# A two-layer graph network on one core: new costs, three dependences and a new order in the planner

## The chip, the core and the metric

The kernel runs on one core of a Trainium2 chip. Its engines work from queues of their own: PE (TensorE, matrix products), DVE (VectorE), ACT (ScalarE), POOL (GpSimd) and SP (SyncE, which here issues nearly all DMA transfers). [...] The metric is the device time of one execution in microseconds (us), as the median of several runs; lower is better. Everything is float32.

## The reference

The input x has 64 batches of 256 tokens with 512 features; adj is one 256 x 256 mask for all. Two layers follow each other, each with a residual and a layer norm:

```
q, k, v = x@Wq+bq, x@Wk+bk, x@Wv+bv                      (8 heads of 64)
attn    = softmax(q k^T / 8, masked with -1e9 where adj is 0)
x       = layernorm(x + (attn v) @ Wo + bo)
h       = x @ W
e       = leaky_relu(h a1 (by rows) + h a2 (by columns), 0.2) * adj
x       = layernorm(x + elu(softmax(e) h + beta h))
```

## The kernel before, in words

**Tiling and rounds.** Batches go in pairs m = 0 to 31; batch s = 0 or 1 is half of a pair. A pair shares x transposed (xT) and the products q, k and v; all else is done per batch. The pieces of work on PE have names: "x" (a gate, see below), "q", "k", "v", and per half "scores00" to "scores31" (head pair c of half s), "sums" (softmax denominators), "mix" (weights times v), "o" (the Wo product), "logits", "attention", "spread" (second-layer weights times x) and "u" (product with W). The table ROUND is the order of these pieces within a round; LATER says how many rounds after (or, negative, before) its own number a pair's piece is done, so that a round mixes pieces of three or four pairs. The last pair is done by the table FINISH, of (piece, how many pairs before the last). take_turn (L601) turns these tables into PE's order.

**Products.** project (L429) computes a matrix product in seven half-size products in place of eight, with sums and differences of quarters. It calls pe(1), pe(5), pe(2), pe(6), pe(3), pe(4), pe(7) in that order. Four PSUM accumulators serve them: chain, cross, second and fourth; for narrow products (o, u, spread) second and fourth are two halves of one tile, "both" (ps_pair in the profile). gather (L480) or onto (L934) move the quarters to SBUF: for q, k, v, spread and u a copy on ACT and an addition on DVE, for o two additions on DVE. token_sums (L408) makes the operand's sums on POOL (xS, oS, yS). PSUM has 8 slots (tag "ps"); x's sums have a single one ("xP").

**Attention.** scores (L758) uses 64-row tiles of PE (mode "rows" in the planner); for each head DVE adds the mask (L774), ACT exponentiates (L776), POOL adds two key halves (L779), and DVE transposes and reduces (L785, L786). denominators (L790) is one 32-column product, L794, then a reciprocal on DVE (L797) and two steps of DMA through DRAM, rows_all and inv_all (L801, L805). mixed (L734) uses 64-column tiles (mode "columns", L744); its result is scaled on DVE (L858). norm (L573) is two passes with row sums on ACT (L580), three small operations on POOL (L591 to L593) and a scaling pass on ACT (L597).

**The planner.** Nothing is emitted at once: plan.op (L90) records engine, an estimated duration, the emitting function, what is read and written, and which buffers are claimed. place (L121) then simulates the engines with these numbers and a fixed latency LAG per engine, and picks operations one by one, by possible start and by a due time that is counted back from PE's order. The order that comes out is emitted engine by engine; on the chip each engine runs its own list in order. Only the last OPEN = 70 products may be reordered on PE. An operation of PE with duration 0 emits nothing: it is a gate, at which buffers of that stage are claimed ("x", "logits", "attention"). A DVE operation with mode "two" isn't planned at the same time as one of POOL, since they share a port ("port" in place). Durations and latencies only shape the order: true waits come from the data.

Of the kernel before, what the change touches and what calls it, by code (L numbers as in the profile page):

```python
# [22 lines left out]
ROUND = ("mix1", "sums1", "scores30", "scores20", "scores00", "scores10", "logits0", "v", "spread1", "o1", "u1", "x",  # L23
         "mix0", "sums0", "scores31", "scores21", "scores01", "scores11", "attention0", "q", "attention1", "logits1",
         "k", "spread0", "o0", "u0")

LATER = {"sums1": 1, "mix1": 1, "scores00": 0, "scores10": 0, "scores20": 0, "scores30": 0, "spread1": 2, "v": 0,
         "u1": 2, "attention0": 1, "sums0": 0, "mix0": 0, "scores01": 0, "scores11": 0, "scores21": 0, "scores31": 0,
         "o1": 1, "x": -2, "logits1": 1, "q": -1, "spread0": 1, "o0": 0, "attention1": 1, "u0": 1, "k": -1, "logits0":
         1}  # L30

FINISH = (("logits0", 1), ("mix1", 1), ("sums1", 1), ("scores00", 0), ("scores30", 0), ("scores20", 0), ("v", 0),
          ("scores10", 0), ("spread1", 2), ("logits1", 1), ("o1", 1), ("scores31", 0), ("sums0", 0), ("u1", 2),
          ("attention0", 1), ("mix0", 0), ("scores01", 0), ("u0", 1), ("scores21", 0), ("attention0", 0),
          ("spread0", 1), ("u1", 1), ("o0", 0), ("spread1", 1), ("spread0", 0), ("logits1", 0), ("logits0", 0),
          ("sums1", 0), ("scores11", 0), ("attention1", 0), ("o1", 0), ("attention1", 1), ("mix1", 0), ("u0", 0),
          ("spread1", 0), ("u1", 0))
# [25 lines left out]
class Plan:  # L63
# [11 lines left out]
    SWITCH = 100.0  # L75
# [14 lines left out]
    def op(self, engine, ns, fn, reads=(), writes=(), mode=None, claims=(), first=False):  # L90
# [24 lines left out]
        self.ops.append((engine, ns, fn, deps, bufs, mode))  # L115
        if engine == "PE":
            self.turns.append((self.turn, n))
        if first:
            self.first = n

    def place(self):  # L121
# [10 lines left out]
        for n in reversed(turns):  # L132
            t += self.SWITCH if ops[n][5] != mode else 0.0
            mode = ops[n][5]
            due[n] = t
            t += ops[n][1]
        for n in reversed(range(len(ops))):
            e, ns = ops[n][:2]
            if e != "PE":
                late = [due[u] - ns - (self.LAG[e] if ops[u][0] != e or e == "SP" else 0.0)  # L140
                        for u in users[n] if due[u] is not None]
                due[n] = min(late, default=None)
# [5 lines left out]
        for n in reversed(range(len(ops))):  # L148
            e, ns = ops[n][:2]
            rest[n] = ns + max((rest[u] + (self.LAG[e] if ops[u][0] != e or e == "SP" else 0.0) for u in users[n]),  # L150
                               default=0.0)
# [17 lines left out]
        while len(order) < len(ops):  # L169
            best = None  # L170
            for e, cand in ready.items():
# [3 lines left out]
                for n in cand:  # L175
                    start = max(now[e], base[n])
                    _, ns, _, _, bufs, m = ops[n]
# [15 lines left out]
                    cost = self.SWITCH if e == "PE" and m != mode else 0.0  # L193
# [7 lines left out]
            _, ns, _, _, bufs, m = ops[n]  # L201
            if e == "PE" and m != mode:
                start += self.SWITCH
                mode = m
            if e == "PE":
                turns.remove(n)
            if e == "POOL" or m == "two":
                port = start + ns
# [5 lines left out]
            now[e] = start + ns  # L214
            end[n] = start + ns + self.LAG[e]
# [6 lines left out]
            for u in users[n]:  # L222
                need[u] -= 1
                lag = 0.0 if ops[u][0] == e and e != "SP" else self.LAG[e]
                base[u] = max(base[u], start + ns + lag)
                if not need[u]:
                    ready[ops[u][0]].append(u)
# [9 lines left out]
def gnn_two_layers(ctx: ExitStack, tc: tile.TileContext, x, adj, Wq, bq, Wk, bk, Wv, bv, Wo, bo, W, a, beta, out):  # L237
# [107 lines left out]
    def transposed_mask():  # L345
# [8 lines left out]
        plan.op("DVE", 690, lambda: nc.vector.tensor_scalar(  # L354
# [19 lines left out]
    def streamed(w, w_dram, name):  # L374
# [16 lines left out]
        def fetch(n):  # L391

            piece = sb("piece", [2, F], f"{name}_{n}")
            if n in raw:
                i, c = raw[n]
                plan.op("SP", 800, lambda: nc.sync.dma_start(
                    piece[A], w_dram[2 * c * P:2 * (c + 1) * P, half(i)].rearrange("(c p) f -> p c f", p=P)), [],
                    [piece])
            else:
                k = {5: 1, 6: 2, 7: 3, 3: 4}[n]  # L400
                plan.op("SP", 800, lambda: nc.sync.dma_start(piece[A].rearrange("p c f -> p (c f)"), kept[k - 1]),
                        [(kept, k)], [piece])
# [26 lines left out]
    def project(left, right, by_feature, claims, copy, add, inner=2, width=P, first=False):  # L429
# [21 lines left out]
        ns = 224 * inner * 2 if by_feature and width == P else 435 * inner * (width // P)  # L451
# [3 lines left out]
        def pe(n, to, start, after=()):  # L455
# [3 lines left out]
            plan.op("PE", ns, lambda: product(n, acc(), start), sides[n][1] + right[n - 1][1] + list(after), [to],  # L459
                    claims=claims)  # L460
# [19 lines left out]
    def gather(quarter, bias=None, wide=False):  # L480

        def copy(q, acc):
# [4 lines left out]
            for f in range(2):  # L487
                plan.op("ACT", 370, lambda f=f: nc.scalar.activation(  # L488
# [3 lines left out]
        def add(q, acc):  # L492
            (dst, key), (src, acc) = quarter(q), acc[::-1]
            plan.op("DVE", 690 if wide else 420, lambda: nc.vector.tensor_add(dst(), src(), dst()), [acc, key], [key])  # L494
# [33 lines left out]
    def residual_bias():  # L528
        bo_sb = for_now(bo, 0, "bo")
        acc, part = ps([D], "ps_b"), sb("half", [D], "bv_wo")  # L530
        for c in range(C):
            plan.op("DVE", 690, lambda c=c: nc.vector.scalar_tensor_tensor(
# [4 lines left out]
            acc[A], ones[:, 16:17].to_broadcast([P, P]), part[A], start=True, stop=True), [part], [acc], claims=[res_sb])  # L537
        plan.op("DVE", 690, lambda: nc.vector.tensor_add(res_sb[A], acc[A], bo_sb[A]), [acc, bo_sb], [res_sb])
# [6 lines left out]
    def second_layer_constants():  # L545
# [4 lines left out]
        for i in range(2):  # L550
            col, a_sb = st(C, "col"), for_now(a, i * D, "a")
            for c in range(C):
                junk = sb("half", [D], "junk")
                plan.op("DVE", 780, lambda c=c, junk=junk, col=col, a_sb=a_sb: nc.vector.scalar_tensor_tensor(  # L554
# [9 lines left out]
            plan.op("DVE", 690, lambda i=i, row=row: nc.vector.tensor_copy(wa_sb[:, i, :], row[A]), [row], [(wa_sb, i)])  # L564
# [8 lines left out]
    def norm(X, ts):  # L573
# [4 lines left out]
        def total(i, t, func, to, bias):  # L578
            junk = sb("half", [D], "junk")
            plan.op("ACT", 700, lambda: nc.scalar.activation(  # L580
# [5 lines left out]
        plan.op("DVE", 110, lambda: nc.vector.tensor_scalar(mean[A], sums[A], -1.0 / D, None, ALU.mult), [sums], [mean])  # L586
# [8 lines left out]
        plan.op("POOL", 1000, rsqrt, [sq, mean], [rs, nm])  # L595
# [12 lines left out]
    def pair(m, at, general=False):  # L608
# [28 lines left out]
        def blocks(s):  # L637
# [3 lines left out]
            for f in range(4):  # L641
                plan.op("SP", 700, lambda f=f: nc.sync.dma_start(
                    xb[f * 32:(f + 1) * 32].rearrange("p c (b i) -> p c b i", i=32), rows[f]), [], [(xb, f)])
# [47 lines left out]
    def batch(m, s, qT, kT, V, dram, general):  # L691
# [12 lines left out]
        def finish(ts, us, u, mode):  # L704

            for t in ts:
                m = sb("half", [D], "m")
                plan.op("ACT", 640, lambda t=t, m=m: nc.scalar.activation(m[A], u(t), AF.Exp), us(t), [m])
                plan.op("DVE", 700, lambda t=t: nc.vector.scalar_tensor_tensor(
                    X[:, t, :], u(t), 0.0, X[:, t, :], op0=ALU.max, op1=ALU.add), us(t), tokens(t), mode=mode)  # L710
                plan.op("DVE", 700, lambda t=t, m=m: nc.vector.scalar_tensor_tensor(  # L711
                    X[:, t, :], m[A], 1.0, X[:, t, :], op0=ALU.min, op1=ALU.add), [m], tokens(t), mode="two")
            norm(X, ts)
            for t in ts:
                plan.op("SP", 700, lambda t=t: nc.sync.dma_start(dram(out, s)[:, t, :], X[:, t, :]), tokens(t), [])
# [10 lines left out]
        plan.op("SP", 2800, lambda: nc.sync.dma_start(X[A], dram(x, s)), [], tokens(0) + tokens(1))  # L726
        for t in range(NT):
            plan.op("POOL", 1270, lambda t=t: nc.gpsimd.tensor_tensor(X[:, t, :], X[:, t, :], res_sb[A], ALU.add),  # L728
# [5 lines left out]
        def mixed(pT, g, onto):  # L734
# [12 lines left out]
            plan.op("PE", 1740, pe, [(V, (g, j)) for j in range(NT)] + pT[4 * g:4 * g + 4], [acc],  # L747
# [3 lines left out]
        def attention_by_keys():  # L751
# [6 lines left out]
            def scores(c):  # L758
# [11 lines left out]
                plan.op("PE", 870, pe, [(m, (c // 2, j)) for m in (qT, kT) for j in range(NT)], acc, mode="rows",  # L770
                        claims=pT[2 * c:2 * c + 2] + ([] if last else [both[c]]))
                for i in range(2):
                    h = 2 * c + i
                    plan.op("DVE", 690, lambda h=h, i=i: nc.vector.tensor_add(pT[h][A], acc[i][A], maskT_sb[A]),  # L774
# [402 lines left out]
```

## Time and profile before

| What | Value |
|---|---|
| median of 3 runs | 2688.45 us (2688.29 to 2689.46) |
| profiled execution, its own time | 2692.57 us |
| its span, first to last instruction | 2690.8 us |
| mean granted clock of PE | 0.997 |
| busy: PE, PE weight loads | 2662.2, 2252.2 us |
| busy: DVE, ACT, POOL | 2212.4, 1483.6, 1688.5 us |
| DMA | 301.21 MB, mean 112 GB/s |

The profile comes from one execution. A line of a timeline gives start, duration, engine, line of code, operation, what is written and read, and how many instructions of a kind follow each other. A matmul's duration includes its pipeline, so the next one starts before its end; what one costs is read from start to start. In the list of waits each line is: who waited, for whom, total us, how often, the longest. "PEld" is the loading of weights into PE. The engine named as the one that ended a wait is inferred.

### The profile page before, as it was taken

The page shows a single profiled execution, that of the slowest core. Times are in us where ns is not written, and L with a number is a line of the kernel's source. Part 1 is how long each engine was busy: PE and PEld are TensorE (multiplying, and loading weights), DVE is VectorE, ACT ScalarE, POOL GpSimd, SP SyncE. Part 2 cuts the span into 40 slices and gives each one's busy share as a digit, 9 for nine tenths or more (in the row PEclk, how much of TensorE's full clock was granted, in tenths as well). Part 3 has the DMA queues.
Part 4 walks back from the last instruction along what each step waited for, and adds up shares of the span by engine and source line. Part 5 has one row for each costly group of instructions (what it writes and reads, how often), then busy time and mean ns, then how long its engine had stood idle before and what let it go on. Part 6 is the DMA issues. An engine that isn't in the chain of part 4 may idle for free.

```text
span 2690.8 us, 45707 instructions
## 1 busy us (share of the span) xinstructions
PE 2662.2 (99%) x15037; PEld 2252.2 (84%) x15037; DVE 2212.4 (82%) x4188; ACT 1483.6 (55%) x3457; POOL 1688.5 (63%) x2254
## 2 busy tenths in 40 slices
PE   8999999999999999999999999999999999999997
PEld 7888888888888888888888888888888888888875
DVE  7878788888888888887878878888888788887886
ACT  3446556455565565564655655556546556455565
POOL 5765666665666655766556666566665666665654
PEclk9999999999999999999999999999999999999998
DMA  8435443454433545334544335443354543453321
GB/s 231 108 99 129 122 122 80 100 138 116 126 96 80 134 120 130 111 78 113 134 116 124 86 96 134 120 126 103 77 126 126 124 116 81 106 138 97 91 79 45
DMA packets 583227, 301.21 MB, mean 112 GB/s; under 512 B 409416, under 2 KB 513864, under 8 KB 582984
## 3 DMA queue, kind: packets, MB, share of 16 engines
q1 hardware_dynamic: 582856, 298.20, 43.1%
q8 instruction: 124, 2.03, 0.3%
q14 instruction: 119, 0.97, 0.1%
q0 software_dynamic: 128, 0.01, 0.0%
HBM read 245.63 MB, written 52.48 MB: 111 GB/s over the span
## 4 chain that ended last, share of the span: by engine, by line
PE 97%; DVE 1%; DMA 0%; issue 0%; ACT 0%; POOL 0%; SPq 0%; POOLq 0%; DVEq 0%
PE ps_chain L448 34%; PE ps_cross L448 22%; PE ps_pair L448 10%; PE ps_sc L767 9%; PE ps_pv L744 8%; PE ps_second L448 6%; PE ps_fourth L448 6%; PE ps_plain L513 0%; DMA xin<-in_x_dram 0%; DVE junk L959 0%; DMA row<-line 0%; PE ps_den L794 0%; DVE junk L554 0%; DVE x L711 0%; PE ps_plain L508 0%
## 5 line engine op out<-in xcount | busy, mean ns | idle before, releaser
L779 POOL TENSOR_TENSOR both<-pT 128x256 f32<-128x256 f32 x504 | 382.6, 786 | 76.8 <-ACT pT L776 74.6
L774 DVE TENSOR_TENSOR pT<-ps_sc,maskT_sb 128x512 f32<-128x512 f32 x512 | 318.3, 676 | 22.3 <-PE ps_sc L767 22.3
L776 ACT ACTIVATE pT<-pT 128x512 f32<-128x512 f32 x512 | 294.1, 624 | 30.9 <-DVE pT L774 30.8
L591 POOL TENSOR_SCALAR rs<-sq 128x2 f32<-128x2 f32 (+1 forms) x130 | 26.2, 202 | 404.8 <-ACT junk L580 402.2
L580 ACT ACTIVATE junk<-x 128x512 f32<-128x512 f32 x256 | 161.2, 630 | 190.4 <-DVE x L936 153.4
L959 DVE SCALAR_TENSOR_TENSOR junk<-x,wa_sb 128x512 f32<-128x512 f32 x256 | 213.8, 862 | 37.6 <-ACT x L597 36.6
L767 PE MATMUL ps_sc<-qT,kT 64*128 64x256 f32 x2048 | 239.6, 383 | 1.8 <-DVE kT L494 1.4
L597 ACT ACTIVATE x<-x,nmr,rs 128x512 f32<-128x512 f32 x256 | 202.6, 810 | 63.6 <-POOL nmr L593 63.6
L744 PE MATMUL ps_pv<-pT,v 128*64 128x256 f32 x2048 | 235.1, 382 | 0.0
L767 PEld LDWEIGHTS ps_sc<-qT,kT 64*128 64x128 f32 x2048 | 192.9, 187 | 25.9 <-DVE kT L494 1.8
L744 PEld LDWEIGHTS ps_pv<-pT,v 128*64 128x64 f32 x2048 | 141.4, 137 | 86.3 <-issue 20.9
L580 ACT ACTIVATE junk<-x,mean 128x512 f32<-128x512 f32 x256 | 183.8, 719 | 9.0 <-DVE mean L586 9.0
L419 POOL TENSOR_TENSOR oS<-oT 128x256 f32<-128x256 f32 x126 | 92.2, 732 | 138.1 <-DVE oT L858 133.2
L785 DVE STREAM_TRANSPOSE flip<-both 128x512 f32<-128x512 f32 x252 | 174.9, 694 | 4.4 <-DVE part L786 0.5
L786 DVE TENSOR_REDUCE part<-flip 128x16 f32<-128x512 f32 x252 | 172.1, 683 | 6.5
L728 POOL TENSOR_TENSOR x<-x,res_sb 128x512 f32<-128x512 f32 x128 | 177.3, 1406 | 0.0
L997 POOL TENSOR_TENSOR e<-e,adj_sb 128x512 f32<-128x512 f32 (+1 forms) x66 | 82.4, 1249 | 140.2 <-DVE e L994 140.2
L485 ACT COPY u<-ps_chain 128x256 f32<-128x256 f32 x126 | 45.0, 357 | 215.3 <-PE ps_chain L448 215.2
L488 ACT ACTIVATE kT<-ps_chain,bk_sb 128x256 f32<-128x256 f32 x128 | 53.8, 472 | 168.6 <-PE ps_chain L448 168.6
L1068 POOL TENSOR_TENSOR att_sums<-attT 128x128 f32<-128x128 f32 x126 | 70.7, 561 | 120.2 <-DVE attT L1032 114.4
L448 PE MATMUL ps_chain<-sw_sb,yS 128*128 128x256 f32 x504 | 132.4, 385 | 0.0
L936 DVE TENSOR_TENSOR x<-x,ps_chain 128x256 f32<-128x256 f32 x252 | 100.2, 417 | 38.0 <-PE ps_chain L448 32.2
(248 smaller groups left out, 7306.5 us busy)
## 6 DMA issues: line engine op xcount, KB each, us to landing
x<-in_x_dram SPq DMA_DIRECT2D x64, 512.0 KB, 3.7
out_dram<-x SPq DMA_DIRECT2D x128, 256.0 KB, 2.1
inv_all<-rows_all SPq DMA_DIRECT2D x126, 256.0 KB, 4.8
xin<-in_x_dram SPq DMA_DIRECT2D x248, 128.0 KB, 3.9
wq_sums<-wq_sums SPq DMA_DIRECT2D x124, 256.0 KB, 2.9
wk_sums<-wk_sums SPq DMA_DIRECT2D x124, 256.0 KB, 4.2
wq_sums<-in_L_gnn_Wq_dram SPq DMA_DIRECT2D x93, 256.0 KB, 4.1
wk_sums<-in_L_gnn_Wk_dram SPq DMA_DIRECT2D x93, 256.0 KB, 4.3
```

Source lines behind the costliest of these rows:

```text
L448: nc.tensor.matmul(dst[:, f, :], lhs, rhs, start=start and f == 0 and c == 0, stop=c == inner - 1, skip_group_check=True)
L580: plan.op("ACT", 700, lambda: nc.scalar.activation(junk[A], X[:, t, :], func, bias=mean[:, i:i + 1] if bias else 0.0, accum_out=to[:, i:i ...
L597: plan.op("ACT", 810, lambda i=i, t=t: nc.scalar.activation(X[:, t, :], X[:, t, :], AF.Identity, bias=nm[:, i:i + 1], scale=rs[:, i:i + 1] ...
L728: plan.op("POOL", 1270, lambda t=t: nc.gpsimd.tensor_tensor(X[:, t, :], X[:, t, :], res_sb[A], ALU.add), [res_sb], tokens(t))
L744: nc.tensor.matmul(acc[r * HD:(r + 1) * HD, i, :], V[:, 2 * k + s, h * HD:(h + 1) * HD], pT[h][:, k, :], start=k == 0, stop=k == NT - 1)
L767: nc.tensor.matmul(acc[j][:, k, :], kT[r:r + HD, c, key_blk(k)], own(qT, r, c), start=True, stop=True)
L774: plan.op("DVE", 690, lambda h=h, i=i: nc.vector.tensor_add(pT[h][A], acc[i][A], maskT_sb[A]), [acc[i], maskT_sb], [pT[h]])
L776: plan.op("ACT", 620, lambda h=h: nc.scalar.activation(pT[h][A], pT[h][A], AF.Exp, scale=1.0 / HD ** 0.5), [pT[h]], [pT[h]])
L779: plan.op("POOL", 725, lambda h=h, i=i: nc.gpsimd.tensor_tensor(both[c][:, i, :], pT[h][:, 0, :], pT[h][:, 1, :], ALU.add), [pT[h]], [(bot ...
L785: plan.op("DVE", 640, lambda: nc.vector.transpose(turned[A], both[c][A]), [both[c]], [turned])
L786: plan.op("DVE", 600, lambda: nc.vector.tensor_reduce(part[:, 2 * c:2 * c + 2, :], turned[A].rearrange("p i (q k) -> p i q k", k=32), AX.X ...
L959: plan.op("DVE", 780, lambda t=t, i=i, junk=junk: nc.vector.scalar_tensor_tensor(junk[A], X[:, t, :], 1.0, wa_sb[:, i, :], op0=ALU.mult, o ...
```

## The change

No arithmetic changes, and no operation or transfer is added or taken away. What changes is the planner and the order that it gives:

- ROUND, LATER and FINISH are new tables. In a round, q of the next pair stands between o1 and u1; the denominators stand ahead of the mix; attention0 and attention1 stand together among the scores of half 1; logits1 behind k; two scores of half 0 end a round and two begin the next. x is prepared one round later than before. The residual bias's product follows ROUND's "x" in round 0, so it moves to a place between two scores.
- An operation may have its own latency ("lag"): SP's transfers have a short occupation and a latency by kind. AFTER is a latency between dependent operations of one engine; KEPT is the end part of an operation in which its engine is already free.
- A change of PE's mode costs by the mode that is left (200 ns from "rows", else 100); gates no longer count as a change; a restart of PE after a wait costs AGAIN = 100. The denominators have a mode "one".
- Dependences: product 4 of project also counts as writing the other half of its PSUM tile, so that it waits in the plan for that half's reader; z (L988) counts as an operation that shares the port with POOL; operations of one engine that depend on each other keep AFTER between them.
- Some fifty durations are set anew.

```diff
-ROUND = ("mix1", "sums1", "scores30", "scores20", "scores00", "scores10", "logits0", "v", "spread1", "o1", "u1", "x",
-         "mix0", "sums0", "scores31", "scores21", "scores01", "scores11", "attention0", "q", "attention1", "logits1",
-         "k", "spread0", "o0", "u0")
+ROUND = ("scores20", "x", "scores10", "v", "logits0", "spread1", "o1", "q", "u1", "sums0", "mix0", "scores11",
+         "scores01", "attention0", "attention1", "scores31", "scores21", "k", "logits1", "spread0", "o0", "u0",
+         "sums1", "mix1", "scores00", "scores30")
...
-FINISH = (("logits0", 1), ("mix1", 1), ("sums1", 1), ("scores00", 0), ("scores30", 0), ("scores20", 0), ("v", 0),
...
+FINISH = (("logits0", 1), ("attention0", 1), ("scores20", 0), ("v", 0), ("spread1", 2), ("scores10", 0), ("o1", 1),
...
     LAG = {"PE": 260.0, "DVE": 70.0, "ACT": 70.0, "POOL": 90.0, "SP": 4200.0}
-    SWITCH = 100.0
+    KEPT = {"PE": 0.0, "DVE": 80.0, "ACT": 95.0, "POOL": 40.0, "SP": 0.0}
+    AFTER = {"PE": 0.0, "DVE": 30.0, "ACT": 30.0, "POOL": 80.0}
+    SWITCH = {None: 100.0, "rows": 200.0, "columns": 100.0, "sums": 100.0, "one": 100.0}
+    AGAIN = 100.0
...
+    def _lag(self, n, u):
+        e = self.ops[n][0]
+        return self.AFTER[e] if self.ops[u][0] == e and e != "SP" else self.ops[n][6]
...
-                    cost = self.SWITCH if e == "PE" and m != mode else 0.0
+                    cost = 0.0
+                    if e == "PE" and ns:
+                        cost = self.SWITCH[mode] if m != mode else self.AGAIN if start > now[e] else 0.0
...
-                port = start + ns
+                port = start + ns - self.KEPT[e]
...
-            now[e] = start + ns
-            end[n] = start + ns + self.LAG[e]
+            now[e] = start + ns - self.KEPT[e]
+            end[n] = start + ns + lag
...
-            plan.op("PE", ns, lambda: product(n, acc(), start), sides[n][1] + right[n - 1][1] + list(after), [to],
-                    claims=claims)
+            plan.op("PE", ns, lambda: product(n, acc(), start), sides[n][1] + right[n - 1][1] + list(after),
+                    [to] + list(after), claims=claims)
...
-                plan.op("ACT", 370, lambda f=f: nc.scalar.activation(
+                plan.op("ACT", 470, lambda f=f: nc.scalar.activation(
...
-        plan.op("POOL", 1000, rsqrt, [sq, mean], [rs, nm])
+        plan.op("POOL", 1250, rsqrt, [sq, mean], [rs, nm])
...
-                    stop=True), [part, fold_sb], [acc], mode="columns", claims=[inv])
+                    stop=True), [part, fold_sb], [acc], mode="one", claims=[inv])
...
-                    plan.op("SP", 1000, spread, [(rows_all, b)], [(everywhere, i)])
+                    plan.op("SP", 660, spread, [(rows_all, b)], [(everywhere, i)], lag=4700)
...
-            plan.op("DVE", 480, lambda t=t: nc.vector.tensor_scalar(
-                z[:, t, :], row[A], sv[:, t, 1:2], None, ALU.add), [row, (sv, (0, t))], [(z, t)])
+            plan.op("DVE", 430, lambda t=t: nc.vector.tensor_scalar(
+                z[:, t, :], row[A], sv[:, t, 1:2], None, ALU.add), [row, (sv, (0, t))], [(z, t)], mode="two")
```

## The prediction

> **What bounds the kernel now.** First the page: busy time per engine, then the chain that ended last.
>
> ```profile
> PE 2662.2 (99%) x15037; PEld 2252.2 (84%) x15037; DVE 2212.4 (82%) x4188; ACT 1483.6 (55%) x3457; POOL 1688.5 (63%) x2254
> PE 97%; DVE 1%; DMA 0%; issue 0%; ACT 0%; POOL 0%; SPq 0%; POOLq 0%; DVEq 0%
> ```
>
> TensorE (PE) sets the end, but "busy" hides small losses: ends of matmuls are modelled and overlap the next start. So I count from start to start. In the chain of waits the scores of batch 1 of two neighbouring rounds begin at
>
> ```profile
> 1906.47 3.65 PE ps_sc L767 x32
> ...
> 1989.10 3.65 PE ps_sc L767 x32
> ```
>
> so a round (one pair of batches) takes 82.63 us. Next the timeline of PE inside that round:
>
> ```profile
> 1926.26 1.03 PE L448 MATMUL ps_cross<-wo_sb,oT 128*128 128x256 f32 x4
> 1927.12 1.03 PE L448 MATMUL ps_pair<-wo_sb,oT 128*128 128x256 f32 x4
> ...
> 1928.85 1.03 PE L448 MATMUL ps_cross<-so_sb,oT 128*128 128x256 f32 x4
> 1929.95 1.10 PE L448 MATMUL ps_pair<-wo_sb,oS 128*128 128x256 f32 x4
> 1930.89 1.03 PE L448 MATMUL ps_chain<-so_sb,oS 128*128 128x256 f32 x4
> ...
> 1934.34 1.03 PE L448 MATMUL ps_chain<-sw_sb,yS 128*128 128x256 f32 x4
> 1935.35 1.13 PE L448 MATMUL ps_cross<-sw_sb,yT 128*128 128x256 f32 x4
> 1936.31 1.03 PE L448 MATMUL ps_pair<-w_sb,yS 128*128 128x256 f32 x4
> 1937.34 1.13 PE L448 MATMUL ps_chain<-sw_sb,yS 128*128 128x256 f32 x4
> 1938.40 3.67 PE L744 MATMUL ps_pv<-pT,v 128*64 128x256 f32 x32
> 1941.90 0.25 PE L794 MATMUL ps_den<-fold_sb,part 128*64 128x32 f32 x2
> 1942.08 3.72 PE L767 MATMUL ps_sc<-qT,kT 64*128 64x256 f32 x32
> 1945.74 1.99 PE L448 MATMUL ps_chain<-xT,wq_sums 128*128 128x256 f32 x8
> ```
>
> An undisturbed product of four matmuls steps by 0.864 (1926.26 to 1927.12). Here two products of o1 take 1.10 + 0.94, so 0.31 too long. Four of u1 take 1.01 + 0.96 + 1.03 + 1.06 = 4.06, which is 0.60 over 3.46; 0.09 of it is a change of tile shape (below), 0.51 is stall. Together 0.82 us a round. Starts in other rounds show the same in o1/u1, first at 194 us, and none in o0/u0. The list of waits agrees in count; the engines behind it come from the DVE and ACT timelines:
>
> ```profile
> PEld ps_pair L448 <- POOL yS L419: 12.5, 28, 0.4
> PEld ps_chain L448 <- ACT u L485: 11.5, 29, 0.4
> 1929.39 0.41 DVE L936 TENSOR_TENSOR x<-x,ps_pair 128x256 f32<-128x256 f32 x1
> 1934.31 0.63 ACT L580 ACTIVATE junk<-x 128x512 f32<-128x512 f32 x1 [1.12 <-DVE x L936]
> 1934.94 0.35 ACT L485 COPY u<-ps_cross 128x256 f32<-128x256 f32 x1
> ```
>
> The o1 wait is put down to POOL, but POOL's yS ended at 1929.54 and the next weight load began at 1929.92, just after DVE's read of the first half of ps_pair ended at 1929.80: product 4 writes the other half of that PSUM tile. The planner knew no such dependence. The u1 wait is ACT: the norm of o1 stood ahead of the copies of u1 and was itself waiting for DVE.
>
> **What the Trainium skill says.** "TensorE: Matmul & The Clock Gate", Architectural detail: ACT and DVE are strict FIFOs; the trace agrees, ACT sat 1.12 us idle with a ready copy behind L580. "TensorEngine Tiling (Array Packing)", Key Properties: changing the tiling mode drains TensorE; the trace agrees, 0.09 to 0.20 us a change. "GPSIMD Engine Reference", Specifications: SBUF interfaces are shared with VectorE operations in two-port mode; L988 (z), which the old plan thought free of this, runs 336 to 1432 ns.
>
> **The change, part by part.**
>
> *Cost of a change of mode.* From starts at 1240.76 to 1250.88: into the mix 0.95 - 0.86 = 0.09, its first pair 3.51 - 3.46 = 0.05, the denominators 0.18 - 0.05 (two 32-column matmuls) = 0.13, scores 3.65 - 3.45 = 0.20, first product after 1.83 - 1.73 = 0.10. Sum 0.57 a half round, 1.14 a round. With 0.82 of stalls that is 1.96; The bare products of a round are q, k, v 3 x 12.09, o and u 4 x 6.05, spread 2 x 3.13, scores and mixes 4 x 3.455, denominators 0.1: 80.65. 80.65 + 1.96 = 82.61 of the 82.63, so nothing else is lost in a round.
>
> *New order, denominators first ("sums", "mix", "scores").* Before, the denominators follow the mix in the same tile shape and cost nothing to enter. Now they are entered from full shape (0.09), and the mix goes straight into scores. That direct change occurs once before, at 2600.70 to 2604.30: 3.60 against 3.51, so +0.10. What the mix costs after two tiny matmuls is not in the trace: between nothing over the bare 0.05 and the 0.23 that they took ahead of a full product at 2594.23. New half: 0.09 + (0 to 0.18) + 0.05 + 0.10 + 0.20 + 0.10 = 0.54 to 0.72 against 0.57. I take +0.08, since the mix's weight load (137 ns) has only 28 ns of matmul to hide under. 61 halves: +4.9 us, ends -1.8 and +9.2.
>
> *New order, q between o1 and u1.* The 12.09 us of q now separate o1's norm (about 4 us of ACT) from u1's copies. u1's stall goes: 29 x 0.51 = -14.8 us. If another ACT item stands there instead, it returns; bound 0.
>
> *Product 4 now depends on the reader of the pair's other half.* The planner places DVE's add earlier in o1: 30 x 0.31 = -9.3 us (bound 0 if DVE is late anyway; it is 68 of 82.6 us busy). No instruction is added for it.
>
> *Durations, transfers, ports, AFTER and KEPT.* These move no work by themselves, only the order on each engine. DVE's z counted as two-port, ACT's 470 for 370, POOL's norm 1250 for 1000, DMA lags 1700 to 4700 for 4200: each is near the measured median (rows_all 1.7, inv_all 4.8, square 2.3 us). Being medians, half of the transfers land later than planned, and DVE, a FIFO, waits with evictions behind it. Now such waits before oT and z are 12.8 us in all, hidden behind matmuls. I allow 0.1 us a round, +3 us, ends 0 and +15.
>
> *Chains that the order shortens.* From denominators of batch 0 to o0: mix0 3.6, scores 3.65, k 12.1, spread0 3.1, so 22.5 us instead of 31. From 1907.5 (reciprocal, two DMAs in a row, scaling on DVE) to the last oS difference on POOL at 1923.2 it took 15.6: room 7. Attention0's gate to spread0: scores and k, 14 us instead of 24, for four issues of 0.65, 2.5 to land, a 0.67 transpose and 2.1 of POOL, 8 us: room 6. Logits1's gate moves behind k, so its line and row transfers stand on SP behind k's fetches, and 12 us nearer to spread1 (34.7 instead of 46.8); its chain, some 21 us by the same rows, still fits. SP issues as many transfers as before. All this costs nothing while PE's other products cover it; past its room, each us late is a us on PE. x's sums: see the rival.
>
> *Start.* ps_b (the residual bias) moves from before mix0 to between two scores of round 0. Its DVE sums ended at 29.5 us, before the scores at 37.8, so it doesn't wait for data, only for a PSUM bank (one eviction, 0.6 to 1.3). Against it, q now gives DVE 12 us before mix0, where scores were stretched from 3.65 to 4.74. Net 0, ends -1.5 and +2.
>
> *Tail.* Behind 2604 us PE loses 1.2, 0.4, 0.4, 0.5, 0.8 and 2.6 us in waits, and then about 2.8 because twelve matmuls run at half pace (L508 steps 0.427, not 0.216, after 2.3 us of idling at 2633.8; "TensorE: Matmul & The Clock Gate", What's actually happening, describes a clock halved after an idle window). The last 12.8 us, norm and store, stay. A plan with truer numbers should lose some of this: I take -2, ends -8 and +5.
>
> Sum: -14.8 - 9.3 + 4.9 + 3 + 0 - 2 = -18.2 us. The span of 2690.8 becomes 2672.6, its execution 2692.6 becomes 2674.4. The runs' median lies 4.1 below that execution, so 2688.45 - 18.2 = 2670.3, or 2670.
>
> **Rivals.**
>
> *Larger gain.* The tail's idling before L508 and the half-pace stretch vanish (-5.4, of which -2 is counted) and no new waits come (-3): 2664; with a free step from denominators to mix (-6.7) 2657. For it: the pace fell through one wait only. Against: the last stages are one dependent chain.
>
> *The stalls move.* Only the planner's picture changes; another item of ACT or DVE stands ahead of an eviction, 0.6 to 0.8 us a round remain, the extra change costs 5: 2686. For it: the old plan also thought it had no stalls.
>
> *Slower: xS late for q.* The sums of x have one buffer, so POOL may write the next pair's only when v's last product has read them. From there q comes after 24 us now (1922.2 to 1945.7), but after spread1 and o1, 9.2 us, in the new order. q's second product, at 11.0, needs two sums of 1.28 and the release, 2.9: room 8.1 us. POOL is a FIFO with oS, yS, "both" and the norms in that stretch (at 1908 to 1922 it was busy 10 of 14 us). If the second sum ends later than 8.1 + 0.6 us behind its best, the stall outweighs the 0.6 a round that the rest gains; at 1.0 us more, 30 rounds give about +12: 2700.
>
> **How the numbers follow.** Likeliest case 0.58 (2661 to 2682: the switch's ends, the waits at 0 to 7), larger gain 0.17, stalls move 0.09, slower 0.16. A measurement of this kernel can tell about 0.2%, 5.4 us: the first two are faster, 0.75; the third is same, 0.09; slower 0.16. For 8 in 10 I cut the far gain below 2652 and the loss above 2694.
>
> **What would show it.** Right: round period of 81.9 to 82.2; o1 stepping 0.864 throughout; u1 too; no "PEld ps_chain <- ACT u" of 29 times; mix to scores about 3.6. Wrong: waits of about 30 times on POOL xS or oS ahead of q or o0, or on attT ahead of spread0; a period of 82.6 or more; a denominators step over 0.25; a tail with a longer stretch at half pace.

## The result, and the profile after

The changed kernel took 2679.37 us (median of 9 runs, 2677.89 to 2681.18) against 2688.29 for the kernel before (2685.38 to 2689.46, 9 runs): a ratio of 0.9969, 95% interval 0.9959 to 0.9979. That is 8.9 us faster, half of the 18.2 that the sum gave. The profiled execution took 2677.89 us with a span of 2676.1.

The page of the kernel after, first busy time per engine, then the chain that ended last:

```profile
PE 2650.1 (99%) x15037; PEld 2314.3 (86%) x15037; DVE 2127.7 (80%) x4188; ACT 1476.8 (55%) x3457; POOL 1649.8 (62%) x2254
PE 98%; DVE 1%; ACT 0%; issue 0%; DMA 0%; POOL 0%; SPq 0%; ACTq 0%; DVEq 0%; POOLq 0%
```

PE still sets the end. In the chain of the kernel after, the denominators of batch 0 begin in two neighbouring rounds at these times:

```profile
1155.06 0.17 PE ps_den L803
...
1237.46 0.17 PE ps_den L803
```

So a round takes 82.40 us, where the prediction's terms per round lead from 82.63 to about 82.07. Next comes PE's timeline of the kernel after at the place that had the stalls: o1, then q, then u1, and into the new switch.

```profile
1263.74 1.03 PE L455 MATMUL ps_cross<-so_sb,oT 128*128 128x256 f32 x4
1264.61 1.03 PE L455 MATMUL ps_pair<-wo_sb,oS 128*128 128x256 f32 x4
1265.47 1.03 PE L455 MATMUL ps_chain<-so_sb,oS 128*128 128x256 f32 x4
1266.33 1.89 PE L455 MATMUL ps_chain<-xT,wq_sums 128*128 128x256 f32 x8
...
1281.87 1.03 PE L455 MATMUL ps_cross<-sw_sb,yT 128*128 128x256 f32 x4
1282.73 1.03 PE L455 MATMUL ps_pair<-w_sb,yS 128*128 128x256 f32 x4
1283.60 1.03 PE L455 MATMUL ps_chain<-sw_sb,yS 128*128 128x256 f32 x4
1284.56 0.24 PE L803 MATMUL ps_den<-fold_sb,part 128*64 128x32 f32 x1
1284.57 0.43 PE L753 MATMUL ps_pv<-pT,v 128*64 128x256 f32 x1
1284.63 0.22 PE L803 MATMUL ps_den<-fold_sb,part 128*64 128x32 f32 x1
1284.69 3.65 PE L753 MATMUL ps_pv<-pT,v 128*64 128x256 f32 x31
1288.27 3.72 PE L776 MATMUL ps_sc<-qT,kT 64*128 64x256 f32 x32
```

Both products of o1 and all of u1 step by 0.86: the stalls are gone. In the mean of 18 rounds in the middle of both traces this is 0.31 us a round in o1 and 0.48 in u1. The two small matmuls of the denominators run between the first ones of the mix; from the first of them to the scores it takes 3.71 us, where the mix and the denominators behind it took 3.68 before. But a product that had no stall before now has one. This is spread0 on PE in the same kernel:

```profile
1223.05 0.61 PE L455 MATMUL ps_chain<-att_sums,X_sums 128*128 128x128 f32 x4
1223.50 0.61 PE L455 MATMUL ps_cross<-attT,X_sums 128*128 128x128 f32 x4
1224.24 0.68 PE L455 MATMUL ps_pair<-att_sums,x 128*128 128x128 f32 x4
1224.76 0.61 PE L455 MATMUL ps_chain<-att_sums,X_sums 128*128 128x128 f32 x4
1225.21 1.03 PE L455 MATMUL ps_chain<-wo_sb,oT 128*128 128x256 f32 x4
```

An undisturbed product of spread steps by 0.45. Product 3 (the second ps_cross) takes 0.74 until product 4 (ps_pair) starts, and that takes 0.52: 0.36 lost. Spread1 loses 0.22; over the same 18 rounds the two together lose 0.54 us a round more than before. DVE's timeline beside it, and the wait of PE's weight load that the list of waits reports:

```profile
1220.20 0.71 DVE L794 STREAM_TRANSPOSE flip<-both 128x512 f32<-128x512 f32 x1 [0.97 <-POOL both L788]
...
1223.08 0.68 DVE L501 TENSOR_TENSOR kT<-ps_chain,kT 128x512 f32<-128x512 f32 x1
1223.68 0.41 DVE L501 TENSOR_TENSOR yT<-ps_pair,yT 128x256 f32<-128x256 f32 x1
```

```profile
PEld ps_pair L455 <- POOL x L737: 8.4, 29, 0.3
```

The addition yT<-ps_pair (L501) reads product 2's half of the pair tile and ends at 1224.09. Product 4, which writes the other half, starts at 1224.24. The list of waits names POOL. Its L737 did end close by, at 1224.00, so the times alone don't decide; but L737 prepares x of another batch, which product 4 doesn't read, and the first experiment below settles it. In the planner's own clock the addition stands 0.34 us earlier against the start of this spread, and leaves product 4 about 0.1 us of room.

The next table has the losses of PE against undisturbed steps, counted from start to start, in us. The numbers of the kernel before come from a second profile of it (the last experiment).

| Stretch | before | after | difference |
|---|---|---|---|
| start, to the seventh mix | 12.53 | 13.27 | +0.7 |
| 26 rounds, to the 59th mix | 56.58 | 51.29 | -5.3 |
| end part | 17.10 | 10.57 | -6.5 |
| last matmul to the end of the span | 12.64 | 12.50 | -0.1 |

The differences sum to -11.2, and the spans differ by 11.1 (2687.2 and 2676.1). The medians differ by 8.9: the profiled execution after lies 1.5 us below its median, the second one of before 0.4 above.

### The profile page after: what moved, and what is told of

It is laid out like the page before. It is cut to its first block, busy times and chain, and to the rows that moved or that the text cites. A ratio compares the mean times of both kernels' runs of the same rounds, so it can differ in the third digit from the quotient of the medians.

```text
span 2676.1 us, 45973 instructions
## 1 busy us (share of the span) xinstructions
PE 2650.1 (99%) x15037; PEld 2314.3 (86%) x15037; DVE 2127.7 (80%) x4188; ACT 1476.8 (55%) x3457; POOL 1649.8 (62%) x2254
## 4 chain that ended last, share of the span: by engine, by line
PE 98%; DVE 1%; ACT 0%; issue 0%; DMA 0%; POOL 0%; SPq 0%; ACTq 0%; DVEq 0%; POOLq 0%
PE ps_chain L455 34%; PE ps_cross L455 22%; PE ps_pair L455 11%; PE ps_sc L776 9%; PE ps_pv L753 8%; PE ps_second L455 6%; PE ps_fourth L455 6%; PE ps_den L803 0%; PE ps_plain L520 0%; DMA wq_sb<-in_L_gnn_Wq_dram 0%; DVE junk L968 0%; ACT junk L588 0%; PE ps_plain L515 0%; PE ps_y L1052 0%; PE ps_plain L517 0%
## 5 line engine op out<-in xcount | busy, mean ns | idle before, releaser
L753 PE MATMUL ps_pv<-pT,v 128*64 128x256 f32 x2048 | 241.1, 382 | 0.0
L968 DVE SCALAR_TENSOR_TENSOR junk<-x,wa_sb 128x512 f32<-128x512 f32 x256 | 231.9, 931 | 1.9 <-ACT x L605 1.8
L1077 POOL TENSOR_TENSOR X_sums<-x 128x256 f32<-128x256 f32 x126 | 135.7, 1092 | 128.3 <-DVE x L719 85.2
L753 PEld LDWEIGHTS ps_pv<-pT,v 128*64 128x64 f32 x2048 | 210.0, 137 | 2.7 <-issue 0.7
L737 POOL TENSOR_TENSOR x<-x,res_sb 128x512 f32<-128x512 f32 x128 | 160.8, 1279 | 0.0
L426 POOL TENSOR_TENSOR yS<-yT 128x256 f32<-128x256 f32 x126 | 92.1, 731 | 66.8 <-DVE yT L501 62.0
L455 PE MATMUL ps_chain<-so_sb,oS 128*128 128x256 f32 x504 | 129.4, 379 | 0.0
L455 PE MATMUL ps_chain<-sv_sb,xS 128*128 128x256 f32 x512 | 120.9, 379 | 0.0
```

The lines of the kernel that those rows point to most:

```text
L455: nc.tensor.matmul(dst[:, f, :], lhs, rhs, start=start and f == 0 and c == 0, stop=c == inner - 1, skip_group_check=True)
L737: plan.op("POOL", 1300, lambda t=t: nc.gpsimd.tensor_tensor(X[:, t, :], X[:, t, :], res_sb[A], ALU.add), [res_sb], tokens(t))
L753: nc.tensor.matmul(acc[r * HD:(r + 1) * HD, i, :], V[:, 2 * k + s, h * HD:(h + 1) * HD], pT[h][:, k, :], start=k == 0, stop=k == NT - 1)
L968: plan.op("DVE", 770, lambda t=t, i=i, junk=junk: nc.vector.scalar_tensor_tensor(junk[A], X[:, t, :], 1.0, wa_sb[:, i, :], op0=ALU.mult, o ...
```

## Experiments

My first theory after the result (A) was that spread's product 4 is held by DVE's read of the other half of its PSUM tile, and that this took back most of what u1 and o1 gave. The rival (B) was a wait that goes with another piece: the order of the pieces, or POOL, as the list of waits has it.

**Own tiles in spread.** The changed kernel with one edit in project:

```diff
-        if width == P:
+        if width == P and inner > 1:
             both = ps([2] + shape, "ps_pair")
```

> The changed kernel, but in spread alone products 2 and 4 have two PSUM tiles of their own in place of the two halves of one. Theory A (spread's product 4 waits for DVE's read of the other half, and DVE comes late because the plan left no margin): the excess of 0.24 and 0.40 us per spread falls to 0.05 or less each, the round from 82.40 to about 81.8, the time by 15 to 18 us to about 2663. Rival B (DVE and ACT are late with every eviction in spread, the tile makes no difference): the wait moves to product 3, 6 or 7, the round stays above 82.2 and the time within 5 us of 2679.

Measured: 2666.35 us (2664.73 to 2666.60), ratio to before 0.9917, interval 0.9903 to 0.9930. The period is 81.82. Spread0 on PE in this kernel:

```profile
1216.13 0.61 PE L455 MATMUL ps_chain<-att_sums,X_sums 128*128 128x128 f32 x4
1216.58 0.61 PE L455 MATMUL ps_cross<-attT,X_sums 128*128 128x128 f32 x4
1217.02 0.61 PE L455 MATMUL ps_fourth<-att_sums,x 128*128 128x128 f32 x4
1217.47 0.61 PE L455 MATMUL ps_chain<-att_sums,X_sums 128*128 128x128 f32 x4
```

Every product steps by 0.45. In a round of the two traces, PE, DVE, ACT, POOL and SP each run the same instructions in the same order; only the shared tile is gone, and with it 0.58 us a round, 15.1 us in the 26 rounds. L737 still stands where it stood, so the wait wasn't for POOL. The cause of the missing gain in the rounds is thereby shown. Theory A had the period; the time fell by 13.0 us, not by 15 to 18, because the end part loses 15.6 us where the changed kernel loses 10.6. The kernel is still faster than both.

**The new order alone.** The kernel before with the new ROUND, LATER and FINISH, and with everything else of the old planner:

```diff
-ROUND = ("mix1", "sums1", "scores30", ...
+ROUND = ("scores20", "x", "scores10", "v", "logits0", "spread1", "o1", "q", "u1", "sums0", "mix0", ...
```

> The kernel before with the new three tables alone; durations, latencies and dependences of the plan as before. If the order is what took away u1's stall (q between o1 and u1), u1 steps by 0.864 here too. Theory A: product 4 of o or spread, which this plan doesn't know to wait, stalls by 0.2 to 0.4 each; round 82.2 to 82.9, time 2672 to 2695. Rival (the costs, not the order, took u1's stall away): u1 loses 0.4 or more again.

Measured: 2709.22 us, ratio 1.0077 (1.0064 to 1.0091), period 83.10. u1's stall is gone, so the order is enough for that. o1's product 4 still loses 0.31, and spread1's product 4 now loses 0.19 more than before. Product 5 of v waits too, and v takes 0.74 us a round longer than before:

```profile
PEld ps_cross L447 <- DVE pT L773: 24.6, 28, 0.9
```

Another 8.4 us are lost before the seventh mix. Theory A's time is missed by 14 us. Yet the planner's own clock has 83.07 us a round for this kernel, with a wait at the start of v: with the old durations the plan itself is no better. The order without the new durations costs more than it gives.

**The new durations alone.** The changed kernel with the old tables, so with all new durations, latencies and dependences:

```diff
-ROUND = ("scores20", "x", "scores10", "v", "logits0", "spread1", "o1", "q", "u1", "sums0", "mix0", ...
+ROUND = ("mix1", "sums1", "scores30", ...
```

> The changed kernel with the three old tables: the new costs and dependences in the old order. Theory A: o1's product 4 is now planned for and loses under 0.1 (before 0.31); u1, next to o1's norm, keeps some of its 0.51. Round 82.2 to 82.5, time 2675 to 2687. Rival (costs do all of it): both stalls vanish, round under 82.0, time under 2672.

Measured: 2958.2 us, ratio 1.1005 (1.0989 to 1.1022), far from what both theories gave. The period is about 92, where the planner's own clock has 81.97. The timeline of DVE and its list of waits in this kernel:

```profile
1338.94 0.23 DVE L992 STREAM_TRANSPOSE svT<-s 128x64 f32<-128x64 f32 x1
...
1351.56 0.62 DVE L998 TENSOR_SCALAR z<-row,s 128x256 f32<-128x256 f32 x2 [6.93 <-DMA row<-line]
```

```profile
DVE z L998 <- DMA row<-line: 185.9, 30, 8.1
```

The transfer of svT's line could go at 1339.2, but SP issued it at 1344.78, behind a row of some 25 other issues that began at 1324; the row followed at 1346.92 and landed shortly before z. DVE takes its work strictly in order (the Trainium skill, "TensorE: Matmul & The Clock Gate", Architectural detail, says so of ACT and DVE; this is the dearest case of it here), so for 6.9 us every eviction behind z waits, and PE behind those. In the mean of a round PE loses 4.9 us in spread0 against undisturbed steps, by such a wait and matmuls at half pace after it. The rest isn't z's: k loses 1.7 us, and in the round shown its waits are for transfers of its own weights; spread1 loses 1.4 at its product 4. Late transfers with DVE waiting in order are what the prediction priced at 0 to 15 us; with the new order such waits don't appear. Neither half of the change is good without the other.

**Without the dependence of product 4.**

```diff
             plan.op("PE", ns, lambda: product(n, acc(), start), sides[n][1] + right[n - 1][1] + list(after),
-                    [to] + list(after), claims=claims)
+                    [to], claims=claims)
```

> The changed kernel without one line: product 4 isn't recorded as writing the pair's other half, so that the plan doesn't know this wait; the wait itself stays on the chip. Theory A: product 4 stalls more often, in o too: round 82.5 to 83.0, time 2682 to 2698. Rival (the plan meets or misses the wait by chance, since its margin is nil): within 4 us of 2679.

Measured: 2692.9 us, ratio 1.0016 (1.0009 to 1.0022). The period is 82.42 with one slow round of 83.26 in it; the others take 82.38, close to the changed kernel's 82.40. In a round all queues have the same order as there, and o1 has no stall here either. So it wasn't the dependence that removed o1's stall. Theory A's time came for another reason than the one it gave, and the rival's time is missed. What the dependence is worth, 13.5 us between the medians, lies in the end part, which loses 26.0 us here and 10.6 with it.

**Own tiles in the kernel before, for o and u.**

```diff
-        if width == P:
+        if width == P and by_feature:
             both = ps([2] + shape, "ps_pair")
```

> The kernel before, with one edit: in the narrow products of o and u (not of spread) the second and the fourth product each have a PSUM tile of their own instead of two halves of one. The planner's own clock gives the same period as before, 81.95 us. Theory A (o1's wait of 0.31 us a round was for the DVE addition that reads the other half of the pair tile, though the list of waits named POOL): o1's wait goes, u1's 0.38 to 0.51 us, which waits for ACT's quarter of u's operand, stays; period 82.62 to about 82.3, time about 2679 (2674 to 2684). Theory B (the wait is really for POOL's quarter sums, as the list of waits says): the wait stays, the time is 2688 within 4.

Measured: 2688.28 us, ratio 0.9998 (0.9990 to 1.0006), period 82.61. The time is theory B's, but not its reason, as PE's timeline of this kernel shows, o1 and then u1:

```profile
1926.63 1.03 PE L448 MATMUL ps_cross<-so_sb,oT 128*128 128x256 f32 x4
1927.50 1.03 PE L448 MATMUL ps_fourth<-wo_sb,oS 128*128 128x256 f32 x4
1928.36 1.03 PE L448 MATMUL ps_chain<-so_sb,oS 128*128 128x256 f32 x4
...
1931.81 1.03 PE L448 MATMUL ps_chain<-sw_sb,yS 128*128 128x256 f32 x4
1933.11 1.13 PE L448 MATMUL ps_cross<-sw_sb,yT 128*128 128x256 f32 x4 [0.27 <-ACT u L485]
```

The order on every queue is that of the kernel before. o1's wait is gone (0.87 and 0.86 a step, not 1.10 and 0.94), so it was for the pair tile, not for POOL. But u1's product 6 now takes 1.30 until product 3 starts, where it took 1.00: the 0.30 that o1 gave is waited for 4 us later, for the same ACT chain. Both theories failed to foresee this. In the kernel before, o1's 9.3 us couldn't be had at all as long as u1 stood next to it.

**u1 next to o1 again.** The changed kernel, one edit in ROUND:

```diff
-... "spread1", "o1", "q", "u1", "sums0", ...
+... "spread1", "o1", "u1", "q", "sums0", ...
```

> The changed kernel with one edit in the order: u1 stands directly behind o1 again, and q behind u1. The planner's own clock shows no difference, 81.72 us a round as for the changed kernel. Theory A (u1 stalled before because o1's norm stood ahead of u1's copies on ACT, and the 12 us of q between them are what removed it): u1 waits again, 0.3 to 0.8 us a round; period 82.7 to 83.2, time 2688 to 2704. Theory B (the new durations alone put ACT's and DVE's work in an order without that wait, as the planner believes; q's place adds nothing): period 82.3 to 82.5, time 2679 within 5.

Measured: 2683.32 us, ratio 0.9980 (0.9972 to 0.9988), period 82.56. PE's list of waits in this kernel:

```profile
PEld ps_chain L455 <- ACT u L492: 14.8, 29, 0.5
```

The 29 waits of the kernel before are back, though the planner's own clock saw no difference (81.72 in both). u1 loses 0.49 us a round; so theory A's wait is right. Its period isn't, because spread0's wait vanished in the same move, and the spreads lose 0.33 us a round less than in the changed kernel. An edit of ROUND makes the planner order all engines anew, and around spread0 DVE and POOL have another order here: the addition ends 2.04 us after spread0's first product starts, where it took 2.38 in the changed kernel. So this run shows what u1's place costs with the lists that go with it, not that place alone. The net is 0.16 a round.

**150 ns more room after DVE.** The changed kernel; in the planner:

```diff
     def _lag(self, n, u):
         e = self.ops[n][0]
+        if e == "DVE" and self.ops[u][0] == "PE":
+            return self.ops[n][6] + 150.0
```

> The changed kernel with the pair tile kept, and one edit in the planner: a product on PE that depends on an operation of DVE is planned 150 ns later than that operation's latency allows. The planner's own clock then gives a period of 81.98 us instead of 81.72. Theory A (product 4 of spread waits because DVE runs 0.2 to 0.35 us later than planned and the plan leaves only 0.1 us): spread's waits fall from 0.57 us a round to 0.2 to 0.35, most of which the longer plan takes back; period 82.1 to 82.4, time 2668 to 2682. Theory B (the waits have another cause, and go with the piece that stands before spread): spread's waits stay at 0.5 to 0.6, period 82.6 or more, time 2684 or more.

Measured: 2680.28 us, ratio 0.9970 (0.9959 to 0.9982), period 82.42, spread's waits as before the edit. Theory A's time holds, but not its reason, for the waits didn't shrink; theory B missed period and time. Around spread0 DVE's list has the same instructions in the same order, the first flip waits the same 0.97 us, and the addition ends 0.15 us before product 4 as in the changed kernel. The longer latency moved the planned start of PE, but it pulled nothing forward on DVE, and it left the chip's wait where it was.

**Measured durations and own tiles.** e_split with three durations set to what the trace of the changed kernel shows:

```diff
-                        plan.op("POOL", 735, lambda h=h, i=i: nc.gpsimd.tensor_tensor(
+                        plan.op("POOL", 775, lambda h=h, i=i: nc.gpsimd.tensor_tensor(
...
-        pool(733, sums[2], x1[0, 0], x1[1, 0], sub, tokens(0), [(S, 3)])
+        pool(960, sums[2], x1[0, 0], x1[1, 0], sub, tokens(0), [(S, 3)])
...
-                plan.op("DVE", 770, lambda t=t, i=i, junk=junk: nc.vector.scalar_tensor_tensor(
+                plan.op("DVE", 900, lambda t=t, i=i, junk=junk: nc.vector.scalar_tensor_tensor(
```

> The changed kernel with own PSUM tiles for the second and fourth product of spread (as in e_split), and three durations in the planner's tables set to what the changed kernel's trace shows: the mask's second addition on POOL 775 instead of 735, the token sums of spread's operand on POOL 960 instead of 733, the second-layer reduction on DVE 900 instead of 770. The planner's own clock gives the same period of 81.72 but a span longer by 15 us than e_split's, at the end. Theory A (with own tiles hardly a wait is left in a round, so better durations have nothing to give there): period 81.7 to 81.9, and the time follows the end part: 2664 to 2682. Theory B (0.1 us of the 0.1 us a round that e_split still loses against its plan comes from these three durations): period 81.75 or less, time 2655 to 2664.

Measured: 2679.35 us, ratio 0.9966 (0.9952 to 0.9979), period 81.82, both as theory A had them. The end part loses 26.6 us in place of e_split's 15.6. These three truer durations gave nothing in a round without waits, and the end part came out longer, as the planner's clock had said of it.

**Denominators behind the mix again.** e_split with sums0 and sums1 behind mix0 and mix1 in ROUND:

```diff
-... "u1", "sums0", "mix0", "scores11",
+... "u1", "mix0", "sums0", "scores11",
...
-         "sums1", "mix1", "scores00", "scores30")
+         "mix1", "sums1", "scores00", "scores30")
```

> The changed kernel with own PSUM tiles for the second and fourth product of spread (as in e_split), and the denominators put back behind the mix in ROUND (sums0 and sums1 after mix0 and mix1). The planner's own clock shows the same period, 81.72 us, and an end 11 us later. Theory A (the denominators ahead of the mix cost 0.03 us more per half than behind it, as the steps of the changed kernel show): period 81.76, 0.06 less than e_split. Theory B (they cost 0.08 more per half, the prediction's term): period 81.66. If the chain from the denominators to o, which is then 3.6 us shorter, becomes late, the period grows instead, with a wait of 30 times for oT or oS. Time: 2666 to 2678, from the end part.

Measured: 2674.04 us, ratio 0.9943 (0.9930 to 0.9957), period 81.81. That is a mean: most rounds take 81.76, theory A's number, and a few take up to 0.4 longer by a wait in o1 that e_split doesn't have. So the place of the denominators is worth 0.03 us a half. The time differs by the end part (20.4 us lost in place of 15.6).

**How many products may be reordered at the end.** e_split with OPEN = 60 and with OPEN = 74:

```diff
-    OPEN = 70
+    OPEN = 60
```

> e_split with the last 60 products instead of 70 free to be reordered on PE at the end. The rounds are e_split's, so the period is 81.82; only the end part differs. The planner's own clock ends 7.2 us later than for e_split. Theory A (the planner's picture of the end part holds): 2671 to 2676. Theory B (its picture doesn't hold there, because it knows nothing of the half-pace stretches of PE after a wait, which cost e_split 5 us at the end): anything between 2658 and 2680, set by whether a wait of over 2 us on PE is followed by many matmuls.

> e_split with the last 74 products instead of 70 free to be reordered on PE at the end. The planner's own clock ends 7.8 us later than for e_split. Theory A: 2671 to 2677. Theory B: anything between 2658 and 2680, as for the run with 60.

Measured: 2667.79 us with 60 (2665.82 to 2667.86) and 2674.88 with 74 (2674.74 to 2677.71), period 81.82 in both. With 74 theory A's range holds; with 60 it misses by 3 us. Theory B's range holds both times, but it is wide. The end parts lose 15.2 and 22.7 us. The planner's clock for the end gives a rough rank, not a time. e_split stays the fastest, with 60 as good as equal.

**The kernel before once more.**

> The kernel before once more, unchanged, for a second profile: it shows how much of what differs between two profiles is the kernel. Both theories: time 2688 within 3, period 82.6 within 0.05, o1 and u1 waits as in the first profile. Open is the end part: if the stretch in which PE's matmuls take twice as long after its waits (0.427 instead of 0.216 us) belongs to the order of the work, it is there again at the same place; if it varies from one execution to the next, the loss after the last full round differs by 2 to 6 us.

Measured: 2688.57 us; the profiled span is 2687.2 where the first was 2690.8, the period 82.60. The end part loses 17.1 us in both profiles, with the half-pace stretch at the same instructions. What differs is the start: 12.5 and 15.6 us lost before the seventh mix.

## Why the prediction was right in direction and wrong in size

The direction and the mechanism at u1 held. The time lies inside the range, but 9 us above the forecast, so the gain is half of what was forecast.

- **u1's stall, -14.8: right.** Measured -0.48 us a round for 0.51. It is gone with the order alone, and 29 waits, 14.8 us in all, come back when u1 stands next to o1. One reading was too strong: of the 1.12 us that ACT sat idle, u's copy was ready for some 0.7, by the modelled end of its product (1933.65).
- **o1's stall, -9.3: right in size, wrong in cause.** The prediction let the planned dependence remove it. It is gone without that dependence too, and it stays with the new order alone, so the rest of the planner's change, its durations and latencies, removed it; which of them wasn't tried. That it was for the pair tile and not for POOL, as the prediction read from DVE's timeline, is shown by the own tiles for o and u. The sum treated the two stalls as independent gains; they weren't: by itself o1's is worth nothing, because u1 waits for it again.
- **The switch, +4.9: too high.** Measured 0.03 us a half, some +1.8 in all. The step "the mix's weight load has only 28 ns of matmul to hide under" failed: the two small matmuls stand among the first of the mix, whose weights are loaded beside them. The Trainium skill, "TensorEngine Tiling (Array Packing)", Key Properties, has the fact that was overlooked: different tiles load and multiply in parallel, and only a change of mode drains. The trace agrees: the first matmul of the mix starts 0.01 us after the first of the denominators.
- **Durations, transfers, ports, 0.1 us a round or +3, ends 0 and +15: the step that failed.** Measured 0.54 us a round, some +16 in 30 rounds. The term was sized from waits for transfers that end late. What came was a wait of PE for DVE at a pair tile. The prediction had found just this coupling in o, where product 2's end and product 4's start lie 1.7 us apart, and didn't look for it in spread, whose products are half as long and leave 0.9 us for an addition on an engine that is busy 80% of the time. The changed plan left product 4 of spread 0.1 us there; DVE was 0.34 late. The wait has more than one parent: spread1's came with the new order alone; spread0's didn't, and it went again when q and u1 changed places.
- **Start, 0: +0.7. End part, -2 with ends -8 and +5: -6.5** in the profiled execution. No half-pace stretch is left there, but that may be luck of this execution (below). The runs of its variants lose 10.6 to 26.6 us in this part, so its gain is the least certain of all.

A round by these terms: -0.31 - 0.48 + 0.06 + 0.54 = -0.19 us, where the periods differ by 0.20. The prediction's had been -0.31 - 0.51 + 0.16 + 0.10 = -0.56. Over 30 rounds the new term alone, some 0.44 us dearer than priced, is 13 us; the end part, 4.5 us better than priced, and the switch, 3.1 better, gave part of it back.

Of the rivals, "the stalls move" was nearest: of 0.79 us a round that o1 and u1 gave, 0.54 are lost again in spread. It isn't the same stall, though: with own tiles it is gone, and no other takes its place (81.82 against a planned 81.72). "xS late for q" didn't come: q's products step by 1.73 throughout. Of "larger gain", the half-pace stretch did go, but the new waits came.

Two points stay open. The first is why DVE is late at spread0. Followed back, the addition is late behind the flip, the flip behind POOL's additions, and those behind the transposition attT, for which POOL waits 1.25 us. Just before attT stand the two scalings of oT:

```profile
1211.83 1.82 DVE L867 TENSOR_TENSOR oT<-oT,inv_all 128x512 f32<-128x512 f32 x2
1213.57 0.70 DVE L1041 STREAM_TRANSPOSE attT<-att_b 128x512 f32<-128x512 f32 x1
1212.12 0.98 POOL L788 TENSOR_TENSOR both<-pT 128x256 f32<-128x256 f32 x1 [0.34 <-ACT pT L785]
```

From the first scaling to attT it takes 1.74 us, in each of 18 rounds, where the plan has 1.20. A POOL addition runs beside the scalings and takes 0.98 where others take 0.74; in the plan it comes after them. So the lateness begins here, by the trace; no run tried it apart.

The second is what starts the half-pace stretch, in which a 128x256 matmul steps by 0.427 us in place of 0.216. The Trainium skill, "TensorE: Matmul & The Clock Gate", HAM oscillation, names idle gaps of PE of over some 3.4 us. The stretch did follow 3.5 us of waits at one place in the kernel before, 4.0 in the run with measured durations and 5.4 in e_split, where it cost 2.9 us (not the 5 that the expectation of the run with 60 names). But the traces show no such limit. Here are the changed kernel and then the run with u1 next to o1, at the same place, with 3.1 us of waits in both:

```profile
2622.00 0.32 PE L984 MATMUL tr_s<-ident,s 128*128 128x128 f32 x1
2624.63 0.32 PE L984 MATMUL tr_s<-ident,s 128*128 128x128 f32 x1 [2.31 <-DVE junk L968]
2625.32 0.67 PE L515 MATMUL ps_plain<-wo_sb,oT 128*128 128x256 f32 x2 [0.37 <-DVE oT L864]
2625.83 0.59 PE L517 MATMUL ps_plain<-wo,oT 128*128 128x256 f32 x2
...
2627.93 0.32 PE L984 MATMUL tr_s<-ident,s 128*128 128x128 f32 x1
2630.55 0.47 PE L984 MATMUL tr_s<-ident,s 128*128 128x128 f32 x1 [2.30 <-DVE junk L968]
2631.24 1.19 PE L515 MATMUL ps_plain<-wo_sb,oT 128*128 128x256 f32 x2 [0.21 <-DVE oT L864]
2632.22 1.06 PE L517 MATMUL ps_plain<-wo,oT 128*128 128x256 f32 x2
```

The starts lie equally far apart up to the first product, yet the first run goes on at full pace and the second at half. In the run with the new order alone, 2.9 us without work were followed by the stretch and 3.1 us elsewhere were not. So the length of a wait alone doesn't decide it here.

## What to carry to other kernels

When one stall of a round is traced to two halves of one tile that are read and written by turns, look at every use of that tile pattern, the one with the shortest products first; there the room is smallest, and here two tiles cost nothing in the rounds, as a slot was free. Don't add up stalls that lie close together behind the same engine: what the first one gives, the second one may take. A planner's table and the order that was tuned with it are one thing, so half of such a change tells little of the whole.

## What was unexpected on the chip

- Two 128x32 matmuls in 64-column mode, ahead of 32 matmuls of 128x256 in the same mode, took 3.71 us with them, against 3.68 behind them; the profile shows them interleaved.
- One transfer issued 5.6 us late on SP held DVE for 6.9 us at one instruction, and some 4.9 of the 9 us that a round grew by were lost in the spread that waited for it.
- With the same waits before them, the same matmuls of the end part ran at half pace in one run and at full pace in another. At 2.9 us a stretch, such a difference is a third of what this change gained.
